# Attention and feed-forward in float32: TensorE products split into two row halves of 64, with the units' products in another order

## The chip, the cores and the metric

The kernel runs on one core of one Trainium2 chip. The metric is device time in microseconds (us). TensorE is called PE here, its weight loads PEld, VectorE DVE, ScalarE ACT, GpSimd POOL, and SyncE, which only issues DMAs in this kernel, SP. A letter q behind an engine's name means its queue.

## The reference, cut to what matters

All arrays are float32; x is 8 x 1024 x 128 (8 batches).

```python
xn = layernorm(x)                                   # per row, eps 1e-5
Q = einsum('bnd,hdk->bhnk', xn, proj_q)             # 8 heads
K = einsum('bmd,dk->bmk', xn, proj_k)               # one key and one value head for all
V = einsum('bmd,dv->bmv', xn, proj_v)
weights = softmax(einsum('bhnk,bmk->bhnm', Q, K), axis=-1)
O = einsum('bhnm,bmv->bhnv', weights, V)
Y = einsum('bhnv,hdv->bnd', O, proj_o)
mid = einsum('amh,ehn->aemn', xn, w1)               # 8 experts, no nonlinearity
ffn = einsum('aemn,enh->amh', mid, w2)
out = x + Y + ffn
```

## The kernel before

The program folds weights once, at its start: `wqk` = proj_q[h] proj_k^T, `wvo` = proj_v proj_o[h]^T, and `wf`, the sum of w1[e] w2[e]. What is left per batch is, for each head, logits = xn wqk xn^T, a softmax, and weights times (xn wvo).

**Units and steps.** A unit u is one head of one batch (64 units). A step i is 128 query rows of a unit, so a unit has 8 steps and the program 512, in the loop at L772. In step i the loop issues, in this order for each engine:

- PE: the logits of step i, 128 x 1024 in two halves (`logits`, L362), into one of two PSUM buffers of the pool `ps_sc`, which are taken in turn. Later in the step, from i = LAG = 12 on, products of an older unit (`run`, L793). Every eighth step the queries of the next unit (`queries`, L802, into `ps_sc` too), and four steps later a quarter of the values of a coming group of four units (`values`, L804, the same).
- DVE: the row maximum of step i (L354), then the 32 x 32 block transpose of the weights of step i-1 (`weights_t`, L377), then the reciprocal of step i's row sums (L370).
- ACT: the exponential of step i out of PSUM (L360), the division (L371), and the copies of queries and values out of PSUM (L305, L323, L324).
- SP: after every fourth transpose, 16 DMAs (L405) that move 32-row blocks between partitions, so that keys come to lie on partitions. The first four steps of a unit give `g0[u]` (two buffers), the last four `g1[u]` (one buffer). Each DMA fills 32 partitions of one of four query blocks; the order is block by block, and within a block the partitions from 0 up.

**The products.** Weights times values is done in a scheme with seven products of half matrices in place of eight. With x1, x2 the two key halves of g0 and y1, y2 those of g1, POOL forms f1 = x1 + x2 (`sum_early`, L423, into a buffer of the tag f), then x1 = y1 - x1 (L428, in place), x2 = f1 - y1 (L429, in place) and f4 = y2 - x2 (L431, tag f). On the values' side seven forms lie in `vfs`, four of them differences that POOL makes (L327 to L330). Each of the seven products is 64 output columns wide and runs over four key blocks c (`product`, L435), into one of four PSUM accumulators, in its lower or upper 64 partitions. `pair` (L461) issues two products that fill both halves of one accumulator: j = 0, 1 is product 4 (weights x2 of before any difference), j = 2 to 5 are the products 2 and 1 (of y2 and y1), j = 6 to 9 are 7 and 5 (x1 and f1), j = 10 to 13 are 6 and 3 (the last x2 and f4). So a unit has 14 pairs. `PAIRS` says how many run in a step: 2, 2, 1, 2.

With n = (i - 12) mod 8 and v = (i - 12) // 8, pairs j = 0, 1 of unit v run at n = 0, j = 2, 3 at n = 1, and so on. The transposes that complete g0 of unit v+1 are issued at n = 0, those that complete its g1 at n = 4. `sum_early` of unit v+1 is issued at n = 6, the three later forms of unit v at n = 0.

**Column halves.** All products that are 128 columns wide are split by `both_halves` (L100) into two of 64 columns, the same width as the products above. Every float32 product leaves two matmul and two weight load records in the trace.

Of the kernel before, what the change touches and what calls it, by code (L numbers as in the profile page):

```python
# [17 lines left out]
def kernel(  # L18
# [78 lines left out]

    banks, pwf = [0], []

    def both_halves(dst, lhsT, rhs, start=True, stop=True):  # L100
        for half in range(2):
            r = ts(half, HP)
            nc.tensor.matmul(dst[r], lhsT=lhsT[:, r], rhs=rhs, start=start, stop=stop)  # L103

# [7 lines left out]

    xs, xns, xnTs, qTs, vfs = {}, {}, {}, {}, {}

# [30 lines left out]
    TURNED = NQ * NB * Q * GN  # L145
    VF = GN * 7 * HC * HP
    s_q = scratch("turned", TURNED)
# [3 lines left out]
    wqT, wvT = wqvT[:, :H], wqvT[:, H]  # L151
    s_v = scratch("vf", VF, batch)
    wo, woT = blocks(s_v[:, : H * P]), blocks(s_v[:, H * P : 2 * H * P])
# [35 lines left out]

    lo, hi = slice(0, HP), slice(HP, P)  # L190
    wqk = const.tile([P, H, P], F32, tag="wqk", name="wqk")
# [5 lines left out]

    def transposed(dst, srcs, name, copy):  # L200
# [94 lines left out]

    def queries(u, first=0, last=S, copy=nc.scalar.copy):
        b, h = divmod(u, H)
        if first == 0:
            qTs[u] = work.tile([P, S], F32, tag="qT", name=f"qT_{u}")
        n = last - first  # L300
        pq = slot(f"pq_{u}") if n == S else bank(f"pq_{u}_{first}")
        for c in range(0, n, GS):
            w = min(GS, n - c)
            both_halves(pq[:, c : c + w], wqk[:, h, :], xnTs[b][:, first + c : first + c + w])
        copy(qTs[u][:, first:last], pq[:, :n])  # L305

    def values(s, c, copy=nc.scalar.copy):

        b, k = divmod(s, 2)
        if c == 0:  # L310
            vfs[s] = batch.tile([P, GN, 7, HC, HP], F32, tag="vf", name=f"vf_{s}")
        vf = vfs[s]
        if s == 0:
            pv = [bank(f"pv_{s}_{c}_{g}") for g in range(2)]
        else:
            both = slot(f"pv_{s}_{c}")
            pv = [both[:, ts(g, GS)] for g in range(2)]
        for g in range(2):
            both_halves(pv[g], xnTs[b][:, ts(c + g * HC, P)], wvo[:, ts(k, GN), :])
        v1, v2 = (t.rearrange("p (h j x) -> p h j x", h=GN, j=2) for t in pv)  # L320
        b11, b21, b22, t4, t1, t2, t3 = (vf[:, :, f, c] for f in range(7))
        b12 = t1
        nc.scalar.copy(vf[:, :, 0:5:4, c], v1)  # L323
        copy(vf[:, :, 1:3, c], v2)  # L324

        def differences(copy):
            nc.gpsimd.tensor_sub(t3, b22, b12)  # L327
            nc.gpsimd.tensor_sub(t1, b12, b11)
            nc.gpsimd.tensor_sub(t2, b22, t1)
            nc.gpsimd.tensor_sub(t4, b21, t2)  # L330

        deferred.append(differences)
        if copy != defer:
            flush(copy)

    sums, es, turned, g0s, g1s, f1s, f4s = {}, {}, {}, {}, {}, {}, {}

    pls, spare = {}, []  # L340

    def logits_half(i, g):
        u, n = divmod(i, NB)
        if g == 0:
            pls[i] = slot(f"pl_{i}")
        both_halves(
            pls[i][:, ts(g, GS)], qTs[u][:, ts(n, P)], xnTs[u // H][:, ts(g, GS)]
        )

    nmaxs = {}  # L350
# [10 lines left out]

    def logits(i):  # L362
        logits_half(i, 0)
        logits_half(i, 1)
        row_max(i)
        exponents(i)
# [17 lines left out]
    def move_blocks(k):  # L384
        src = turned.pop(k)
        u, g = divmod(k, 2)
        if u < B * H - 1 or g == 1:
            f = g if u < B * H - 1 else 0
            dst = work.tile(
                [P, NQ, NB, GN, Q], F32, tag=f"g{f}", name=f"g{g}_{u}", bufs=2 - f  # L390
            )
        else:
            spare.append(scratch("vf", VF, batch))
            dst = spare[0][:, :TURNED].rearrange(
                "p (r c t q) -> p r c t q", r=NQ, c=NB, t=GN
            )
        (g1s if g else g0s)[u] = dst

        def ends_of(r, d):
            return dst[ts(d, Q), r], src[ts(r, Q), d]  # L400

        for r in range(NQ):
            for d in range(NQ):
                if d != r or k < NS // GN - 1:
                    nc.sync.dma_start(*ends_of(r, d))  # L405
        if k == NS // GN - 1:
            for r in range(NQ):
                (nc.scalar.copy if r else nc.vector.tensor_copy)(*ends_of(r, r))
# [4 lines left out]
    def form(name, u):  # L413
        return work.tile([P, NQ, HC, GN * Q], F32, tag="f", name=f"{name}_{u}")

    def sum_early(u, engine):
        if u < B * H - 1:
            f1s[u] = form("f1", u)
        else:
            f1s[u] = spare[0][:, TURNED : TURNED + TURNED // 2].rearrange(  # L420
                "p (r c x) -> p r c x", r=NQ, c=HC
            )
        engine.tensor_add(f1s[u], key_half(g0s[u], 0), key_half(g0s[u], 1))  # L423

    def sums_late(u, engine):
        x1, x2 = key_half(g0s[u], 0), key_half(g0s[u], 1)
        y1, y2 = key_half(g1s[u], 0), key_half(g1s[u], 1)
        engine.tensor_sub(x1, y1, x1)  # L428
        engine.tensor_sub(x2, f1s[u], y1)  # L429
        f4s[u] = form("f4", u)  # L430
        engine.tensor_sub(f4s[u], y2, x2)  # L431

    accs = {}

    def product(u, p, c):  # L435
# [3 lines left out]
        x1, x2 = key_half(g0s[u], 0), key_half(g0s[u], 1)  # L439
        y1, y2 = key_half(g1s[u], 0), key_half(g1s[u], 1)  # L440
        acc, half, f, w = {
# [3 lines left out]
            4: (3, c // 2, 3, x2),  # L445
            5: (1, 1, 4, f1s[u]),
            6: (2, 0, 5, x2),
            7: (1, 0, 6, x1),
        }[p]
        first, last = (0, HC - 1) if p != 4 else (2 * half, 2 * half + 1)  # L450
        if (b, acc) not in accs:
            accs[b, acc] = ps_acc.tile([P, GS], F32, tag=f"acc{acc}", name=f"acc{acc}_{b}")
        nc.tensor.matmul(  # L453
            accs[b, acc][ts(half, HP)],
            lhsT=vfs[u // GN][:, u % GN, f, c, :],
            rhs=w[:, :, c, :],
            start=(h == 0 and c == first),
            stop=(h == H - 1 and c == last),
        )

    def pair(u, j):  # L461

        if j < 2:
            product(u, 4, j)
            product(u, 4, j + 2)
        else:
            k, c = divmod(j - 2, HC)
            for p in ((2, 1), (7, 5), (6, 3))[k]:
                product(u, p, c)

# [7 lines left out]

    def ffn(b, k):

        xn0, xn1 = xnTs[b][:, :GS], xnTs[b][:, GS:]
        terms = (
            ((0, lo, xn1), (1, hi, xn0)) if k == 0 else ((3, lo, xn0), (2, hi, row_diffs.pop(b)))
        )
        for acc, half, rows in terms:
            nc.tensor.matmul(  # L486
                accs[b, acc][half],
                lhsT=wf[:, half],
                rhs=rows.rearrange("d (t r q) -> d r t q", t=GN, q=Q),
                start=False,  # L490
                stop=False,
            )

    def in_order(t):
# [240 lines left out]

    PAIRS = (2, 2, 1, 2)
    LAST_PAIRS = (2, 2, 1, 1, 1, 1, 1, 1, 1, 1, 1, 0)
    COLLECT = {0: [0], 2: [1], 3: [2, 3], 4: [4], 6: [5], 7: [6, 7, 8], 8: [9], 10: [10], 11: [11]}

# [11 lines left out]
    LAST = B * H - 1  # L751
    for u in range(LAST - 2):
        jobs.extend((pair, u, j) for j in range(14))
        if u % H == H // 2 and u // H < B - 1:
            jobs.extend((ffn, u // H, k) for k in range(2))

    jobs.extend((pair, LAST - 2, j) for j in range(11))
    jobs.extend((pair, LAST - 1, j) for j in range(2))
# [8 lines left out]
    def run(n):  # L767
        for _ in range(n):
            job, *args = jobs.pop()
            job(*args)  # L770

    for i in range(NS):  # L772
        m = i % GN
        if i == 1:
            exponents(1)
        elif i > 1:
            logits(i)
        for task in early.get(i, ()):
# [8 lines left out]

        v, n = divmod(i - LAG, NB)
        if n == 6 and 0 <= v + 1 < LAST - 1:
            sum_early(v + 1, nc.gpsimd)  # L790


        if i >= LAG:  # L793
            run(
                (PAIRS[m] if i < NS - LAG else LAST_PAIRS[i + LAG - NS])
                + (n == 0 and v % H == H // 2 + 1 and v // H < B - 1) * 2
            )
            if n == 0 and v < LAST - 1:
                sums_late(v, nc.gpsimd)
            elif n == 7 and v + 1 == LAST - 1:  # L800
                sum_early(v + 1, nc.gpsimd)
        if i % NB == 0 and i > 0 and i // NB + 1 < B * H:  # L802
            queries(i // NB + 1)
        if i % NB == GN and i >= LAG:  # L804
            s, r = divmod(i + 20, 32)
            if s < 2 * B:
                values(s, r // NB)

# [77 lines left out]
```

## Time and profile before

| | |
|---|---|
| time, median of 3 runs (least to most) | 1912.9 us (1912.8 to 1914.85) |
| span of the profiled execution | 1911.0 us |
| median less span | 1.9 us |
| granted TensorE clock | 1.000 |
| PE busy, matmul records | 1905.4 us, 8994 |
| DVE, ACT, POOL busy | 1410.2, 1356.1, 1402.1 us |
| DMAs of L405: issues, us from issue to landing | 2044, 2.4 (median) |
| starts of the logits of n = 4, 5, 6, 7 and the next n = 0, 1, in order of time | 1010.12, 1015.27, 1018.71, 1021.28, 1024.71, 1029.87 us |

The profiled execution is one run; its span goes from the first to the last instruction, and the runs' times are a little longer than a span. In the rows quoted below, a matmul row gives line, engine, output <- inputs and sizes (128*64 is 128 rows of the array by 64 columns). The end of a matmul is modelled, its start is recorded; a row of 0.592 us is 0.429 us of streaming, after which the next one of the same column half starts, and 0.163 us in which the last results come out. Square brackets at the end of a row tell how long the engine was idle before it and what ended that.

### The profile page before, as it was taken

What the parts mean: (1) busy time and instruction counts of PE and PEld (TensorE: products, weight loads), DVE (VectorE), ACT (ScalarE), POOL (GpSimd) and SP (SyncE); (2) the same over time, 40 slices, a digit from 0 to 9 for tenths busy, and PEclk for the clock granted to TensorE, in tenths of its full rate; (3) what the DMA queues carried; (4) which work ended last, traced back from release to release, by engine and by line L of the source; (5) the groups of instructions that cost most, each with busy time, mean ns of one, the idle gap of its engine ahead of it and who ended that gap; (6) DMA issues with size and microseconds to landing.
All of it is one profiled execution on the core that took longest, in us unless ns stands there. A gap on an engine that the chain in (4) does not pass through costs nothing.

```text
span 1911.0 us, 26803 instructions
## 1 busy us (share of the span) xinstructions
PE 1905.4 (100%) x8994; PEld 646.3 (34%) x8994; DVE 1410.2 (74%) x1779; ACT 1356.1 (71%) x1823; POOL 1402.1 (73%) x592
## 2 busy tenths in 40 slices
PE   9999999999999999999999999999999999999999
PEld 4333333333333333333333333333333333333333
DVE  8767778677786777777777776777678766787777
ACT  7677677776776777777676777777777776777674
POOL 2877877688676886777967768777687777677763
PEclk9999999999999999999999999999999999999999
DMA  6666676676767766677667776776767667666675
GB/s 200 155 154 148 143 155 153 144 171 150 158 141 156 171 150 147 151 159 167 145 147 158 158 166 138 157 158 144 179 139 156 149 148 173 137 144 146 155 174 133
DMA packets 140713, 295.07 MB, mean 154 GB/s; under 512 B 41120, under 2 KB 74656, under 8 KB 140064
## 3 DMA queue, kind: packets, MB, share of 16 engines
q1 hardware_dynamic: 139744, 292.96, 68.2%
q8 instruction: 72, 1.18, 0.3%
q14 instruction: 65, 0.53, 0.1%
q10 hardware_dynamic: 832, 0.39, 0.1%
HBM read 13.76 MB, written 4.19 MB: 9 GB/s over the span
## 4 chain that ended last, share of the span: by engine, by line
PE 78%; POOL 9%; SPq 5%; DVE 3%; ACT 2%; DMA 2%; issue 1%; POOLq 0%; DVEq 0%
PE pl L103 37%; PE acc L453 32%; SPq L405 5%; PE pq L103 4%; PE pv L103 4%; POOL f L431 2%; POOL g L428 2%; POOL g L429 2%; DMA g<-turned 2%; DVE nmax L354 1%; ACT e L360 1%; DVE turned L377 1%; PE acc L486 1%; ACT e L371 1%; DVE scratch_vf L224 0%
## 5 line engine op out<-in xcount | busy, mean ns | idle before, releaser
L103 PE MATMUL pl<-xnT,qT 128*64 128x512 f32 x4096 | 966.5, 592 | 0.5 <-DVE xnT L294 0.2
L354 DVE TENSOR_REDUCE nmax<-pl 128x1 f32<-128x1024 f32 x512 | 626.3, 1223 | 403.6 <-PE pl L103 402.6
L360 ACT ACTIVATE e<-pl,nmax 128x1024 f32<-128x1024 f32 x512 | 570.1, 1113 | 399.9 <-DVE nmax L354 399.9
L453 PE MATMUL acc<-g,vf 128*64 128x512 f32 x2536 | 843.3, 592 | 0.0
L371 ACT ACTIVATE e<-e,rinv 128x1024 f32<-128x1024 f32 x512 | 588.1, 1149 | 116.5 <-DVE rinv L370 116.4
L377 DVE STREAM_TRANSPOSE turned<-e 128x1024 f32<-128x1024 f32 x512 | 633.8, 1238 | 13.7 <-ACT e L371 2.2
L103 PEld LDWEIGHTS pl<-xnT,qT 128*64 128x64 f32 x4096 | 292.8, 137 | 585.5 <-issue 534.3
L453 PE MATMUL acc<-f,vf 128*64 128x512 f32 x1016 | 487.2, 592 | 0.0
L428 POOL TENSOR_TENSOR g<-g,g 128x2048 f32<-128x2048 f32 x63 | 287.1, 4558 | 260.8 <-DMA g<-turned 127.1
L453 PEld LDWEIGHTS acc<-g,vf 128*64 128x64 f32 x2536 | 247.6, 137 | 506.5 <-issue 503.9
L423 POOL TENSOR_TENSOR f<-g 128x2048 f32<-128x2048 f32 x63 | 287.2, 4558 | 174.3 <-PE acc L453 86.2
L431 POOL TENSOR_TENSOR f<-g,g 128x2048 f32<-128x2048 f32 x63 | 287.8, 4569 | 4.9
L429 POOL TENSOR_TENSOR g<-f,g 128x2048 f32<-128x2048 f32 x63 | 286.9, 4554 | 0.0
L453 PEld LDWEIGHTS acc<-f,vf 128*64 128x64 f32 x1016 | 139.2, 137 | 0.0
L103 PE MATMUL pq<-xnT,wqk 128*64 128x512 f32 (+1 forms) x516 | 121.5, 589 | 0.1
L103 PE MATMUL pv<-wvo,xnT 128*64 128x512 f32 x512 | 120.8, 592 | 0.0
L370 DVE RECIPROCAL rinv<-sums 128x1 f32<-128x1 f32 x512 | 83.8, 164 | 42.9
L360 ACT ACTIVATION_READ_ACCUMULATOR e<-pl,nmax 128x1 f32 x512 | 98.3, 192 | 0.0
L327 POOL TENSOR_TENSOR vf<-vf 128x256 f32<-128x256 f32 x64 | 46.9, 733 | 31.1 <-ACT vf L324 31.1
L305 ACT COPY qT<-pq 128x1024 f32<-128x1024 f32 (+2 forms) x66 | 63.6, 963 | 0.0
L103 PEld LDWEIGHTS pv<-wvo,xnT 128*64 128x64 f32 x512 | 37.2, 137 | 72.7 <-issue 69.4
L103 PEld LDWEIGHTS pq<-xnT,wqk 128*64 128x64 f32 x516 | 36.9, 137 | 71.9 <-issue 71.3
(100 smaller groups left out, 534.0 us busy)
## 6 DMA issues: line engine op xcount, KB each, us to landing
g<-turned SPq DMA_DIRECT2D x2028, 128.0 KB, 2.4
xn<-in_L_attn_x_dram SPq DMA_DIRECT2D x7, 512.0 KB, 4.6
xnT<-xnt SPq DMA_DIRECT2D x112, 32.0 KB, 1.9
out<-yt SPq DMA_DIRECT2D x112, 32.0 KB, 1.9
x<-in_L_attn_x_dram SPq DMA_DIRECT2D x6, 512.0 KB, 4.2
out_dram<-x SPq DMA_DIRECT2D x6, 512.0 KB, 5.1
scratch_g<-in_L_ffn_w_dram SPq DMA_DIRECT2D x2, 1024.0 KB, 8.4
scratch_f<-in_L_ffn_w_dram SPq DMA_DIRECT2D x2, 1024.0 KB, 12.6
```

The lines of the kernel that those rows point to most:

```text
L103: nc.tensor.matmul(dst[r], lhsT=lhsT[:, r], rhs=rhs, start=start, stop=stop)
L354: nc.vector.reduce_max(nmaxs[i], pls[i], AX.X, negate=True)
L360: nc.scalar.activation(es[i], pl, AF.Exp, bias=nmax, accum_out=sums[i])
L370: nc.vector.reciprocal(rinv, sums.pop(i))
L371: nc.scalar.mul(es[i], es[i], rinv)
L377: nc.vector.transpose(turned[k].rearrange("p k c t q -> p c k t q")[:, :, :, j, :], es.pop(i).rearrange("p (c k q) -> p c k q", k=NQ, q=Q),)
L405: nc.sync.dma_start(*ends_of(r, d))
L423: engine.tensor_add(f1s[u], key_half(g0s[u], 0), key_half(g0s[u], 1))
L428: engine.tensor_sub(x1, y1, x1)
L429: engine.tensor_sub(x2, f1s[u], y1)
L431: engine.tensor_sub(f4s[u], y2, x2)
L453: nc.tensor.matmul(accs[b, acc][ts(half, HP)], lhsT=vfs[u // GN][:, u % GN, f, c, :], rhs=w[:, :, c, :], start=(h == 0 and c == first), st ...
```

## The change

PE gets 64-row halves of every product in the steady steps (i = 15 to 499). A product of 128 rows becomes one of the lower 64 rows (start flag as before) and one of the upper 64 that is added to it in PSUM. `couple` issues one half of the rows of two things at a time: the upper rows of one and the lower rows of the other, which write different PSUM banks. At its second call for the same key, it issues the other halves. Ahead of each such call, from the third on, PE gets an instruction that waits until the call before the last one has finished.

```diff
+    def halves(dst, lhsT, rhs, start=True, stop=True):
+        return [(dst[r], lhsT[:, r], rhs, start, stop) for r in (ts(0, HP), ts(1, HP))]
+    def half_rows(job, r, first):
+
+        for dst, lhsT, rhs, start, stop in job:
+            done = nc.tensor.matmul(
+                dst, lhsT=lhsT[r], rhs=rhs[r], start=start and first, stop=stop and not first
+            )
+        return done
+
+    begun, slots = {}, []
+
+    def couple(key, jobs):
+
+        if len(slots) > 1:
+            wait = nc.tensor.nop()
+            tc.add_manual_dep(wait.ins, slots[-2].ins.name, AFTER, reason="other rows of a bank")
+        if key not in begun:
+            begun[key] = jobs
+            half_rows(jobs[1], hi, True)
+            slots.append(half_rows(jobs[0], lo, True))
+        else:
+            a, b = begun.pop(key)
+            half_rows(b, lo, False)
+            slots.append(half_rows(a, hi, False))
```

`queries`, `values`, `logits_half`, `product`, `pair` and `ffn` are rewritten to return lists of such jobs, which `whole` issues as before (used in steps 0 to 14 and from 500 on). In the steady steps the order is

```diff
+    PAIRS = {
+        0: ((0, 2), (-1, 11)),
+        1: ((0, 3), (-1, 12)),
+        2: ((0, 4), (-1, 13)),
+        3: ((0, 5), (0, 6)),
+        4: ((0, 7), (1, 0)),
+        5: ((0, 8), (1, 1)),
+        6: ((0, 9), (0, 10)),
+    }
+    FIRST_PAIRS = (0, 2), (1, 3), (4,)
...
+        def products(own):
+            if n < 7:
+                pairs = [pair_job(v + d, j) for d, j in PAIRS[n]]
+            couple("own", own)
+            if n == 7 and other is None:
+                couple("pairs", None)
+                couple("own", None)
+                return
+            couple("other" if n == 7 else "pairs", other if n == 7 else pairs)
+            couple("own", None)
+            if n == 7:
+                couple("other", None)
+            elif other is not None:
+                couple("other", other)
+                couple("pairs", None)
+                couple("other", None)
+            elif n < 6 or (v % H == H // 2 + 1 and v // H < B - 1):
+                couple("pairs", None)
```

where (d, j) is pair j of unit v + d, `own` is the two halves of the step's logits, and `other` is the values (n = 0), the queries (n = 4) or, once a batch, the feed-forward products (n = 7). The second halves of a pair may so come after the second halves of the logits, and the pairs of n = 6 end at n = 7. The first pairs of unit v+1 (product 4) now run at n = 4 and 5 of unit v, those of y1 and y2 at n = 0 to 3, and the last three pairs of unit v-1 at n = 0 to 2 of unit v. A step's row maximum and exponential are issued after all of this.

The forms follow that order:

```diff
     def sum_early(u, engine):
-        if u < B * H - 1:
+        if in_place(u):
+            f1s[u] = key_half(g0s[u], 1)
+        elif u < B * H - 1:
             f1s[u] = form("f1", u)
...
     def sums_late(u, engine):
...
-        engine.tensor_sub(x1, y1, x1)
-        engine.tensor_sub(x2, f1s[u], y1)
-        f4s[u] = form("f4", u)
-        engine.tensor_sub(f4s[u], y2, x2)
+        if not in_place(u):
+            engine.tensor_sub(x1, y1, x1)
+        f2s[u] = form("f2", u) if in_place(u) else x2
+        engine.tensor_sub(f2s[u], f1s[u], y1)
+        f4s[u] = form("f4", u)
+        engine.tensor_sub(f4s[u], y2, f2s[u])
+
+    def sum_middle(u, engine):
+        x1, y1 = key_half(g0s[u], 0), key_half(g1s[u], 0)
         engine.tensor_sub(x1, y1, x1)
...
+        elif steady():
+            if n == 0:
+                sum_middle(v, nc.gpsimd)
+            elif n == 2:
+                sums_late(v, nc.gpsimd)
+            elif n == 5 and in_place(v + 1):
+                sum_early(v + 1, nc.gpsimd)
```

`in_place(u)` holds for all units but the first and the last three. f1 takes the place of x2, and what was x2 = f1 - y1 goes to a buffer of the tag f as f2. The values' forms `vfs` become two fixed tiles with the key block as the first index; which differences POOL makes is as before. In the last twelve steps the order of pairs (`LAST_PAIRS`) and of the reads of the accumulators (`COLLECT`) is shifted to start with the three pairs that are left over from before.

## The prediction

> **What bounds the kernel now.** I read the page first: busy time of the engines and the granted clock.
>
> ```profile
> PE 1905.4 (100%) x8994; PEld 646.3 (34%) x8994; DVE 1410.2 (74%) x1779; ACT 1356.1 (71%) x1823; POOL 1402.1 (73%) x592
> ...
> PEclk9999999999999999999999999999999999999999
> ```
>
> PE is busy for 1905.4 of 1911.0 us, and the table of matmul groups gives it 0.5 us of idle time ahead of the logits (L103 pl). A busy PE may still hide gaps, so I looked at its weight loads and its matmuls in order of time, in the step that starts at 1010.12 (start us, us, engine, line, operation).
>
> ```profile
> 1010.12 1.89 PE L103 MATMUL pl<-xnT,qT 128*64 128x512 f32 x8
> 1011.84 0.59 PE L453 MATMUL acc<-g,vf 128*64 128x512 f32 x1
> 1011.85 0.59 PE L453 MATMUL acc<-f,vf 128*64 128x512 f32 x1
> 1012.27 0.59 PE L453 MATMUL acc<-g,vf 128*64 128x512 f32 x1
> 1012.28 0.59 PE L453 MATMUL acc<-f,vf 128*64 128x512 f32 x1
> ...
> 1013.56 1.89 PE L103 MATMUL pq<-xnT,wqk 128*64 128x512 f32 x8
> 1015.27 1.89 PE L103 MATMUL pl<-xnT,qT 128*64 128x512 f32 x8
> ```
>
> Every product leaves two records (4096 logits records for 512 steps of four products of 64 columns). Two records of different column halves start 0.01 us apart, and the next two 0.429 us later. So eight records take 1.716 us (1010.12 to 1011.84), gaplessly: PE streams at a fixed pitch. Then I followed one half of the softmax weights from the logits to POOL (DVE, SP and POOL in the same stretch).
>
> ```profile
> 1012.22 1.23 DVE L354 TENSOR_REDUCE nmax<-pl 128x1 f32<-128x1024 f32 x1
> 1013.48 1.25 DVE L377 STREAM_TRANSPOSE turned<-e 128x1024 f32<-128x1024 f32 x1
> ...
> 1014.86 10.04 SPq L405 DMA_DIRECT2D g<-turned  x16
> ...
> 1027.13 4.57 POOL L428 TENSOR_TENSOR g<-g,g 128x2048 f32<-128x2048 f32 x1 [4.47 <-DMA g<-turned]
> ```
>
> The transpose that completes a half stands on DVE behind the same step's row maximum. It ends at 1014.72; sixteen DMAs follow, 0.63 us apart on SP; POOL, which waits for them, starts 12.4 us after the transpose. This half is g1, and its first product comes at 1031.58, 4.5 us after it has landed. g0 has longer. That margin is what I watch.
>
> **The change, part by part.** Durations are those of the profiled execution (span 1911.0 us); the median of the runs shown, 1912.9, is 1.9 above, and I carry that along.
>
> *The matmuls.* Each product becomes two of 64 rows, so 64-row records double and weight loads too. Call one call of couple a slot: half the rows of two products, eight records of the 64 x 64 kind. No row here shows row halves. Below, nothing in the trace gives a pitch shorter than 0.429 for two records, so a slot takes 2 x 0.429 = 0.858 us if its four quarters run side by side; above, 1.716 if the row halves take turns. I take 0.858, since column halves, the nearest row, do run side by side. PE's work per unit is then unchanged: 34 slots (6 in n=0 and n=4, 4 in n=1, 2, 3, 5, 3 in n=6 and 7), 34 x 0.858 = 29.17 us, just what 136 records cost before.
>
> The Trainium skill (FP8 and Floating Point Precision, TensorE Precision Notes) says that true fp32 takes four passes through the array; with the 2.4 GHz of its page TensorE: Matmul & The Clock Gate (table at the top) that makes 853 ns for 128 x 128 x 512, an estimate, and the trace's two pitches, 858 ns, agree, so by it there is nothing to win in streaming. The same skill (TensorE: Matmul & The Clock Gate, Part 3) tells of four row tiles that ran 3.07 times as fast, not four; by that share a slot would take some 1.12 us and the kernel some 2450 us, an estimate that no run here shows.
>
> *Doubled weight loads.* A load takes 0.137 us, and two start together. Four beside each other cost nothing; one after the other they take 0.55 us against a pitch of 0.43, so a slot would be 1.10 us and a unit 37.3. I take nothing.
>
> *The waits.* Ahead of each slot PE waits for the slot before the last one. That slot ends 0.592 - 0.429 = 0.16 us after its streaming, while the next one still has 0.7 us to stream, and the semaphore instruction is a 51 ns row of which some 600 stand in the trace with PE idle for under 1 us. I take nothing; if PE's queue did not run ahead, 34 x 0.21 = 7.3 us a unit, 440 us in all.
>
> *The PSUM slots of the logits.* The second half of a step's logits is now a slot of pairs later, so the step's rows end 2.57 us after it starts, not 1.72. From there: 0.21 to the maximum, 1.22, 0.04, exponential 1.11, 0.14 until PE runs again (least gap in the trace): 2.72 us. At n=1, n=5 and the next n=0 the buffer wanted is that of the step before, 3 slots = 2.57 us after it was filled: 0.15 us late each. These lie ahead of the next two waits and vanish in them.
>
> *The order of the units' products* is the dearest part. The transposes that complete g0[u] and g1[u] stay in the steps n=0 and n=4 of unit u-1, but their first products move: product 4 of u from n=0 of u to n=4 of u-1, the products of y1 and y2 from n=1 to n=0. Both are now four steps after the transpose. From a pairs slot P1 that had to wait, the path to the next one is: P1 and second half of the logits 2 x 0.858 = 1.72; 0.21; maximum 1.22; 0.03; transpose 1.24; landing 12.4: 16.8 us. PE has 18 slots from P1 of n=0 to P1 of n=4, 15.44 us: **1.35 us late**. From P1 of n=4 to that of the next n=0 it has 16 slots, 13.73 us; there the first product in need takes the lower 64 rows, which the first 14 DMAs fill, 2 x 0.63 earlier: 15.5 us, **1.76 late**. A unit costs 29.17 + 3.1 = 32.3. If PE waits for all sixteen there, 1.3 more.
>
> Sum: 61 times 1.35, 60 times 1.76, less 1.7 in each of the seven units that have two ffn slots at n=7 in the way: 82 + 106 - 12 = 176 us. 1911.0 + 176 + 1.9 = 2089, say **2090 us**.
>
> *POOL and SP.* POOL keeps its four forms of 4.56 us. f2 and f4 now start after n=2 of their unit (f2's buffer is read until then) and end at 1.8 + 12.0 + 9.1 = 22.9 us of the unit; g1 has one buffer, whose next DMAs want to start at 23.9. The cover is 1.0 us; each us beyond it moves the landing. They are used at 28. x1, in place, is done 4.6 us after g1 has landed, at 8.6, and used at 14.6. f1 in place frees a buffer and costs nothing. SP has 16 x 0.63 = 10 us in 14: it doesn't queue. The last twelve steps keep whole products and the first pairs at step 12 come after the landing: nothing.
>
> **Rivals.**
> 1. *The row halves take turns.* A slot is 1.716, a unit 58.3: 1913 + 61 x 29.2 = 3690 us. For it: no row shows 64-row tiles beside each other. Against: column halves do it. Between lie serialised weight loads (1913 + 61 x 8.1 = 2410) and bare waits (2355); here landings are hidden again (PE alone decides from a slot of 0.95 us).
> 2. *The landing is no wait*: DMAs land earlier, or the transpose doesn't stand behind the maximum. Then the 0.15 us of the PSUM slots remain, 0.45 a unit: 1940 us, or no change at 1913 if they go too. Against: the 12.4 us are measured, and POOL's wait for them is a row (127 us in total).
> 3. *Faster: 64-row tiles stream quicker.* Place: every slot; price 34 x 61 = 2074 slots, so each 0.01 us less is worth 21 us, if nothing waits. By the path above a unit is 28.8 + 4 slots, which at half the pitch is still 30.5, or 1995 us. Faster than before only if slots shrink below 0.85 and the landings also come 3 us a unit earlier: 29.17 must be undercut. 1880 us if both held and slots took 0.84.
>
> **How the numbers follow.** Landing waits as worked out, 2000 to 2200: 0.57. Dearer slots, 2200 to 2420: 0.12. Turns, 3690: 0.09. Landing mostly hidden, 1917 to 2000: 0.10. Within 0.2%: 0.05. Faster: 0.07. 0.2% is about what a measurement of this kernel can tell from no change. The likeliest is 2090; 1930 to 2400 takes in the sixteen-DMA bound (2170), bare waits and nearly all of the serialised loads, and leaves out turns, no change and faster, 0.2 together.
>
> **What would show it.** Right: matmul records nearly doubled, four with starts within some 0.03 us and 0.43 us between such groups; PE idle of 1 to 2 us ahead of products that read g, put down to the DMAs g<-turned, about twice a unit, some 170 us in all; DVE, ACT and POOL busy as before; units 32 us apart. Wrong: groups of two with 0.43 us between them (turns); PE idle ahead of every slot (bare waits); loads one after another; or no idle and 29.2 us a unit. POOL's f4 ending after the transpose of n=4 would make the landing wait longer than I have it.

## The result, and the profile after

The changed kernel takes **2190.1 us** (median of 4 runs, 2187.07 to 2195.35), beside 1913.1 for the kernel before (1912.8 to 1914.85, 4 runs): 1.1448 times as long, interval 1.1432 to 1.1465. The forecast was 2090, with a range of 1930 to 2400. The direction and the mechanism were right; the loss is 277 us where 176 were worked out. The profiled execution has a span of 2185.3 us, 274.3 more than before, and those 274 us are what is accounted for below.

The page after, busy times and the chain that ended last:

```profile
PE 2028.7 (93%) x17282; PEld 737.7 (34%) x17282; DVE 1415.7 (65%) x1779; ACT 1356.2 (62%) x1823; POOL 1403.8 (64%) x592
...
SPq 40%; PE 36%; DMA 12%; issue 5%; DVE 5%; POOL 1%; ACT 1%; DVEq 0%; POOLq 0%
```

DVE, ACT and POOL do what they did before, and PE's records have nearly doubled. What bounds the kernel has changed, as the chain of before shows beside it: there PE had 78% and SP's queue 5%; now SP's queue has 40% and the DMAs' landing 12%.

```profile
PE 78%; POOL 9%; SPq 5%; DVE 3%; ACT 2%; DMA 2%; issue 1%; POOLq 0%; DVEq 0%
```

PE's matmuls in order of time, in a stretch of step n=0 to 1 without a wait (start us, us, engine, line, operation):

```profile
1214.27 0.60 PE L117 MATMUL acc<-f,vf 64*64 64x512 f32 x2
1214.29 0.60 PE L117 MATMUL acc<-g,vf 64*64 64x512 f32 x2
1214.70 0.60 PE L117 MATMUL acc<-f,vf 64*64 64x512 f32 x2
1214.71 0.59 PE L117 MATMUL acc<-g,vf 64*64 64x512 f32 x2
1215.13 1.04 PE L117 MATMUL pl<-xnT,qT 64*64 64x512 f32 x8
1215.99 0.59 PE L117 MATMUL acc<-g,vf 64*64 64x512 f32 x2
```

Four quarters of the array start within 0.02 us, the next four 0.43 us later, and a slot of eight records takes 0.86 us (1214.27, 1215.13, 1215.99). So the row halves run side by side, at the pitch of before.

Then the path from one waiting product to the next, in the timeline of all engines (g0, the half that is used at n=4):

```profile
1207.12 1.02 PE L117 MATMUL acc<-f,vf 64*64 64x512 f32 x4
...
1208.83 0.65 PE L117 MATMUL acc<-g,vf 64*64 64x512 f32 x2 [0.69 <-DMA g<-turned]
...
1210.85 1.22 DVE L409 TENSOR_REDUCE nmax<-pl 128x1 f32<-128x1024 f32 x1 [1.92 <-PE pl L117]
...
1211.99 1.23 DVE L435 STREAM_TRANSPOSE turned<-e 128x1024 f32<-128x1024 f32 x1
...
1213.29 10.95 SPq L463 DMA_DIRECT2D g<-turned  x16
...
1226.12 1.09 PE L117 MATMUL acc<-g,vf 64*64 64x512 f32 x8 [1.37 <-DMA g<-turned]
```

From product to product (1208.83 to 1226.12) it is 17.29 us, where the forecast had 16.8; PE has 15.44 us of work for that stretch. The sixteen issues on SP take 10.95 us here and took 10.04 in the stretch of before that the prediction shows.

The groups of instructions give the sum of such waits ahead of products that read g:

```profile
L117 PE MATMUL pl<-xnT,qT 64*64 64x512 f32 x7760 | 1066.5, 597 | 3.3
L117 PE MATMUL acc<-g,vf 64*64 64x512 f32 x4856 | 890.5, 595 | 143.6 <-DMA g<-turned 127.4 <-issue 8.0 <-DVE rinv L428 3.8
```

143.6 us look like less than 274. They are idle time of the whole of PE, and in a waiting slot of n=0 two quarters have other work: only the rows of g wait, while those of the other pair, which are issued first (the row at 1207.12), go ahead. So the 1.71 us from 1207.12 to 1208.83 count as 0.69 us of idle time, and PE's "busy" 2028.7 us hide the rest. The sure measure is the distance from one row maximum to the next, since each follows its logits directly:

| from step to step | slots x 0.858 | before | after | difference from PE's work |
|---|---|---|---|---|
| n=1 to 2, 2 to 3, 5 to 6 | 4 = 3.43 | (other order) | 3.43 | 0 |
| n=0 to 1 and n=4 to 5 | 6 = 5.15 | 5.31, 5.32 | 5.40, 5.43 | 0.25, 0.28: PSUM buffer |
| n=3 to 4 | 4 = 3.43 | 3.43 | 5.23 | 1.80: g0 |
| n=6 to 7 | 3 = 2.57 | (other order) | 2.68 | 0.11: one more slot in the seven units with ffn |
| n=7 to 0 | 3 = 2.57 | 3.39 | 4.63 | 2.06: g1, and the same ffn slot |
| sum of a unit (mean) | | 29.44 | 33.66 | 4.22 more than before |

The steps of before hold other products, four slots from n=7 to 0 for example, so its rows compare with the changed kernel's only in the sum.

### The profile page after: what moved, and what is told of

It reads as the page before. It is cut to its first block, busy times and chain, and to the rows that moved or that the text cites. A ratio compares the mean times of both kernels' runs of the same rounds, so it can differ in the third digit from the quotient of the medians.

```text
span 2185.3 us, 44147 instructions
## 1 busy us (share of the span) xinstructions
PE 2028.7 (93%) x17282; PEld 737.7 (34%) x17282; DVE 1415.7 (65%) x1779; ACT 1356.2 (62%) x1823; POOL 1403.8 (64%) x592
## 3 DMA queue, kind: packets, MB, share of 16 engines
q8 instruction: 140, 2.29, 0.5%
## 4 chain that ended last, share of the span: by engine, by line
SPq 40%; PE 36%; DMA 12%; issue 5%; DVE 5%; POOL 1%; ACT 1%; DVEq 0%; POOLq 0%
SPq L463 40%; PE acc L117 15%; DMA g<-turned 12%; PE pl L117 11%; PE pv L117 6%; PE pq L117 2%; DVE nmax L409 2%; DVE turned L435 2%; PE pl L109 1%; PE acc L109 0%; ACT e L429 0%; ACT e L415 0%; POOL f L496 0%; POOL g L492 0%; POOL g L494 0%
## 5 line engine op out<-in xcount | busy, mean ns | idle before, releaser
L117 PE MATMUL pl<-xnT,qT 64*64 64x512 f32 x7760 | 1066.5, 597 | 3.3
L117 PE MATMUL acc<-g,vf 64*64 64x512 f32 x4856 | 890.5, 595 | 143.6 <-DMA g<-turned 127.4
L117 PE MATMUL acc<-f,vf 64*64 64x512 f32 x1928 | 501.8, 589 | 0.0
L117 PEld LDWEIGHTS pl<-xnT,qT 64*64 64x64 f32 x7760 | 301.5, 133 | 585.7 <-issue 414.4
L486 POOL TENSOR_TENSOR g<-g 128x2048 f32<-128x2048 f32 x60 | 273.6, 4561 | 292.9 <-PE acc L117 275.3
L117 PEld LDWEIGHTS acc<-g,vf 64*64 64x64 f32 x4856 | 241.2, 133 | 510.9 <-issue 375.5
L496 POOL TENSOR_TENSOR f<-g,f 128x2048 f32<-128x2048 f32 x60 | 271.8, 4530 | 4.7
L117 PEld LDWEIGHTS acc<-f,vf 64*64 64x64 f32 x1928 | 139.5, 133 | 155.1 <-issue 121.2
L117 PE MATMUL pv<-wvo,xnT 64*64 64x512 f32 x944 | 173.1, 596 | 0.0
L117 PE MATMUL pq<-xnT,wqk 64*64 64x512 f32 x976 | 132.2, 599 | 0.0
```

The costliest lines, as they stand in the source:

```text
L117: done = nc.tensor.matmul(dst, lhsT=lhsT[r], rhs=rhs[r], start=start and first, stop=stop and not first)
L496: engine.tensor_sub(f4s[u], y2, f2s[u])
```

## The experiments

Each time is the median of its runs beside runs of the kernel before on the same chip (1913.1 to 1913.7); "waits at n=4 and n=0" are read as in the table above. A DMA issue of SP has a median of 0.59 us in every kernel; one over 0.8 us is called long.

### e1: the new order, whole rows

```diff
-            begun[key] = jobs
-            half_rows(jobs[1], hi, True)
-            slots.append(half_rows(jobs[0], lo, True))
+            begun[key] = (jobs, fresh)
+            whole(jobs[fresh])
...
-            half_rows(b, lo, False)
-            slots.append(half_rows(a, hi, False))
+            whole(js[1 - k])
```

Here `fresh` picks the first pair, at n=4 the pair of product 4.

> The new order of products with whole rows of 128: no row halves, no added waits, matmul records back to about 9,000. Theory A (the order puts each landing on the path, and doubled instruction fetches lengthen it): PE still waits about twice a unit for the DMAs that move g. With the landing of before (12.4 us) the wait at n=4 is 16.8 - 15.44 = 1.35 us as forecast, and at n=0 it is 16.8 - 13.73 = 3.1 us, since a whole product needs all sixteen DMAs; 61 x 4.4 = 270 us on 1913, and some 10 for the start and the end: 2160 to 2230 us, by chance about the time of the changed kernel. SP's long issues and the instruction packets go back to about 62 and 72. Rival B (row halves or the waits ahead of each slot cost the time): 1913 to 1940 us.

Measured: **2242.5 us**, ratio 1.1723 (1.1681 to 1.1764). Without any row half and any added wait the kernel is slower still, so B falls: the order costs the time. The waits are 1.22 us at n=4 and 3.45 at n=0, 4.67 together where 4.4 were expected; the time is 12 us above the upper end. The surplus shows in PE's clock. Busy times by window, with the granted clock behind POOL's column, and PE's matmuls in the middle window:

```profile
1016.63:1023.46 6.83, 4.90 (x22) 1.20 (x18) 5.45 (x8) 5.29 (x9) 5.68 (x2) 1.00 0.77 169
1023.46:1030.29 6.83, 5.08 (x12) 1.65 (x14) 1.36 (x2) 0.99 (x2) 4.51 (x1) 0.50 0.12 26
1030.29:1037.10 6.81, 6.81 (x34) 2.50 (x32) 3.44 (x4) 4.21 (x6) 2.90 (x4) 1.00 0.63 140
```

```profile
1025.21 1.98 PE L109 MATMUL acc<-g,vf 128*64 128x512 f32 x4 [3.68 <-DMA g<-turned]
1026.94 1.95 PE L109 MATMUL pl<-xnT,qT 128*64 128x512 f32 x4
1028.65 1.86 PE L109 MATMUL pv<-wvo,xnT 128*64 128x512 f32 x4
1030.33 1.04 PE L109 MATMUL acc<-f,vf 128*64 128x512 f32 x4
```

After a wait of 3.68 us the next three slots take 1.68 to 1.73 us in place of 0.86: the clock is at half. Over the whole execution it is at half for 126 us (32 stretches, mean clock 0.972), at most 63 us of lost streaming; in the changed kernel for 27 us.

### e2 and e9: the new order with twice as many instructions

Two ways to cut a matmul in two without row halves. e2 cuts the 512 columns at 256, e9 takes the first and the second 64 queries of each of the four query blocks:

```diff
+            for k in range(2):
                 for dst, lhsT, rhs, start, stop in job:
...
-                nc.tensor.matmul(dst, lhsT=lhsT, rhs=rhs, start=start, stop=stop)
+                    nc.tensor.matmul(
+                        strip(dst, k),
+                        lhsT=lhsT,
+                        rhs=strip(rhs, k),
+                        start=start and k == 0,
+                        stop=stop and k == 1,
+                    )
```

> The kernel of the run before with each matmul of the steady steps cut into two of 256 columns, so that PE's instructions double, without row halves and without added waits. Theory A: about 140 instruction packets, about 110 long SP issues, each landing some 0.6 us longer than in the run before, so 1.2 us a unit, 50 to 90 us more than that run, if a matmul of 256 columns streams in half the time of one of 512. Rival B (instruction fetches don't touch SP; row halves are what made the landing longer): the time and the long issues of the run before. If the pitch of the smaller matmuls is longer than 0.215 us, PE's own work grows, and that part is to be taken off first.

Measured: **2223.5 us** (1.1632, 1.1596 to 1.1667): neither theory's number, but 19 us less than e1. SP did what A said (143 packets, 82 long issues where e1 has 32, the sixteen issues 0.38 to 0.40 us longer at each landing). Why the time fell all the same I could only argue: the first 256 columns read two query blocks, which the first eight DMAs fill, so half of the first product runs before the landing ends. e9 takes that way out:

> Again the new order with whole rows and each matmul cut into two, but the weights' products are cut so that both parts read all four query blocks (the first and the second 64 queries of each), so that the first part can't start before all sixteen DMAs, as it could in the run with two blocks each (there the first part needed eight). Theory A (doubled instructions lengthen SP's sixteen issues, and that lengthens the time): about 140 packets, 80 to 110 long issues, each landing 0.4 us longer than with uncut products, 61 x 0.8 = 49 us and 11 us for the pitch of the smaller matmuls (as the kernel before showed it when it was cut): 2275 to 2325 us beside 2242 for the uncut order. Rival B (the longer issues don't reach the time): 2235 to 2260 us.

Measured: **2294.6 us** (1.2007, 1.1981 to 1.2033), 52 us above e1, as A had it (60), and beyond B. 141 packets, 84 long issues, each landing 0.37 to 0.41 us longer than in e1. Some 11 of the 52 us are the pitch (3.45 us for four slots in place of 3.43). The waits grew from 1.22 and 3.45 us to 1.48 and 3.89, 0.70 together, which times 58 units is about the other 41 us. The clock was at half for 169 us, 43 more than in e1; the half clock that follows a wait is part of these distances, so how much of the 41 us is the clock's is not taken apart.

### e3: the kernel before, with twice as many instructions

The same cut at 256 columns, in `both_halves` and `product` of the kernel before.

> The kernel before, in its own order, with each matmul of the loop cut into two of 256 columns: PE's instructions double. Theory A: about 140 instruction packets in place of 72, about 110 long SP issues in place of 62, the sixteenth issue some 0.5 us later after the transpose; the time stays at 1913 us within 0.3%, since there the landing has 4.5 us to spare. Rival B (fetches and long issues only happen to fall together): packets double and long issues stay near 62. If the smaller matmuls stream slower, the time grows by that alone.

Measured: **1924.2 us** (1.0059, 1.0044 to 1.0074). The time is outside the 0.3%, by the pitch: a unit takes 29.35 us in place of 29.18, times 64 is 11 us. On SP the theory held. With e1, e9 and the changed kernel:

| kernel | instruction packets | long SP issues | first to sixteenth issue, mean us, g0 and g1 |
|---|---|---|---|
| before | 72 | 62 | 9.85, 9.76 |
| before, cut (e3) | 142 | 109 | 10.03, 10.21 |
| new order, whole (e1) | 72 | 32 | 9.78, 9.64 |
| new order, cut (e9) | 141 | 84 | 10.15, 10.05 |
| changed kernel | 140 | 111 | 10.28, 10.14 |
| changed kernel, only pairs in halves (e10) | 101 | 82 | 9.98, 10.02 |

The packets are rows of the table of DMA queues, of before and of after:

```profile
q8 instruction: 72, 1.18, 0.3%
```

```profile
q8 instruction: 140, 2.29, 0.5%
```

Each is 16 KB. That they are PE's instructions is read from their number, which doubles with PE's records (8994 matmuls and as many loads before, 17282 of each after). In the changed kernel 108 of 111 long issues fall together in time with such a packet, in the kernel before 57 of 62; of the other issues it is 53 of 2199 and 32 of 2248. The doubling in e3 and e9, with nothing else changed for SP, makes this more than a coincidence. How many packets meet an issue depends on the order too: e1 has the 72 packets of before and only 32 long issues. Where landings have time to spare (e3) it costs nothing, where they set the end (e9) it does.

### e4: three quarters of the moved blocks

```diff
             for d in range(NQ):
+                if r == NQ - 1 and steady() and 3 < u < B * H - 1:
+                    continue
                 if d != r or k < NS // GN - 1:
```

The tiles of g0 and g1 are then kept from unit to unit.

> The changed kernel, with row halves, waits and order as they are, but in the steady steps the four DMAs of the last of the four query blocks are left out (that block keeps an older unit's weights), so twelve DMAs move each half. Theory A: the landing is 4 x 0.63 = 2.5 us shorter, which is more than the wait at n=4 (some 2.0 us) and at n=0 (some 2.3 us): the waits for g go, the short ones for PSUM buffers (0.19 us, three a unit) stay, 1913 + 35 and some for the start and the end: 1935 to 1970 us. Rival B (row halves, the doubled weight loads or the added waits cost the time): 2150 to 2190 us, since none of them is touched.

Measured: **1991.4 us** (1.0405, 1.039 to 1.0421). B falls: with row halves, doubled loads and waits all there, 199 of the 277 us are gone. The waits for g are 0.03 us at n=4 and some 0.2 at n=0. The group of products that read g has 16.1 us of idle time in place of 143.6, and the chain that ended last is PE's again:

```profile
L117 PE MATMUL acc<-g,vf 64*64 64x512 f32 x4856 | 877.8, 590 | 16.1 <-DMA g<-turned 13.1 <-POOL g L496 1.9 <-issue 1.1
...
PE 90%; SPq 3%; ACT 2%; DVE 1%; POOL 1%; DMA 1%; issue 1%; ACTq 0%; DVEq 0%; POOLq 0%
```

It is 21 us above the upper end. A unit is 30.31 us where before had 29.44: the waits for PSUM buffers are 0.25 us, not 0.19, at n=1, n=5 and n=0, and 61 x 0.87 = 53; the rest are the first two units and the last steps, which stay as slow as in the changed kernel.

### e5: lower rows first at n=4

```diff
-        4: ((0, 7), (1, 0)),
+        4: ((1, 0), (0, 7)),
```

> The changed kernel with the two pairs of n=4 swapped, so that the first slot of product 4 takes the lower 64 rows of g0, as the first slot of n=0 does with g1. Theory A (the first product waits for the last DMA of those rows that it reads): the wait at n=4 then ends with the fourteenth DMA, not the sixteenth, some 1.28 us earlier in each of 61 units: 78 us less, about 2110 us (2090 to 2140), and the wait at n=0 is as before. Rival B (PE waits for a whole transfer, or for something else that ends there): 2190 us.

Measured: **2120.8 us** (1.1079, 1.1062 to 1.1095), 69 us less by swapping two pairs of one step. A's number; B falls. The wait at n=4 fell from 1.80 to 0.41 us, and the one at n=0 rose from 2.06 to 2.29. The idle time of the group:

```profile
L117 PE MATMUL acc<-g,vf 64*64 64x512 f32 x4856 | 935.5, 595 | 62.7 <-DMA g<-turned 53.9 <-issue 4.8 <-POOL g L492 2.2
```

So each product waits for the DMAs of its own rows and no more: the first product starts 2.6 us after the sixteenth issue at n=4 of the changed kernel, and 2.6 us after the fourteenth at n=0.

### e7: the DMAs of the lower partitions first

```diff
-        for r in range(NQ):
-            for d in range(NQ):
+        for d in range(NQ):
+            for r in range(NQ):
                 if d != r or k < NS // GN - 1:
```

> The run with the two pairs swapped, and the sixteen DMAs in another order: the partitions outside, the query blocks inside, so that the first eight fill the lower 64 partitions of all four blocks. Theory A: the first slot waits for eight DMAs, 13 - 8 issues or some 3.2 us earlier than in the run before, and the slot that needs all sixteen comes three slots, 2.57 us, later. At n=4 nothing is late, at n=0 some 1.1 us: 1913 + 67, with the waits for PSUM buffers and the start and end 2000 us (1970 to 2040). Rival B (the sixteen DMAs must all be there before any product starts): 2110 to 2190 us.

Measured: **2008.3 us** (1.0498, 1.048 to 1.0515), as A had it, with everything moved and computed. No wait is left at n=4 (3.44 us for its 3.43), 0.07 us at n=0 beside the PSUM buffer's 0.26, and from n=0 to 1 it is 5.93 us: the slot with the upper rows, 0.78 us late with the PSUM wait in it. The group, with 5.8 us of its idle time put down to the DMAs:

```profile
L117 PE MATMUL acc<-g,vf 64*64 64x512 f32 x4856 | 932.6, 591 | 14.3 <-DMA g<-turned 5.8 <-issue 3.1 <-POOL g L492 2.2
```

### e6 and e8: transposes ahead of the maximum

```diff
+        if ahead(i):
+            weights_t(i - 1)
         nmaxs[i] = small.tile([P, 1], F32, tag="nmax", name=f"nmax_{i}")
```

`ahead` is true in the steady steps with n=0 and n=4.

> The changed kernel with the transposes that complete a half put ahead of the row maximum of the same step on DVE, in the steps n=0 and n=4. Theory A (the path runs from one waiting product through the end of the logits, the maximum and the transpose to the next landing): the transpose no longer waits for the logits of a step that was itself delayed. It can start after the division of the step before, some 4.3 us after that step's logits, so the two waits of a unit together fall from some 4.4 to some 2.0 us: 2045 us (2010 to 2100). Rival B (PE's waits come from the row halves or from SP alone): 2190 us or more, since the maximum now comes later.

> Both together: transposes ahead of the maximum in n=0 and n=4, the DMAs of the lower 64 partitions first, and the lower rows first in n=4. Theory A: what is late at n=0 falls from 1.1 to some 0.4 us and nothing at n=4; with the waits for PSUM buffers 1930 to 1980 us, and not under 1911, since PE's work is 29.17 us a unit as before. Rival B: row halves would also save streaming time once nothing waits: below 1900 us.

Measured: **2211.3 us** (1.1554, 1.1537 to 1.1571) and **2210.0** (1.1549, 1.1532 to 1.1566). Both numbers of A were wrong by 160 us and more. B's number fits e6, and so does its remark that the maximum now comes later; what it says of the waits does not, and e8's B (below 1900) falls too. The waits for g are nearly gone, and a new one has their place. The group of logits and of products, idle time and releaser last:

```profile
L117 PE MATMUL pl<-xnT,qT 64*64 64x512 f32 x7760 | 1043.2, 599 | 183.9 <-ACT e L415 182.7
L117 PE MATMUL acc<-g,vf 64*64 64x512 f32 x4856 | 890.1, 595 | 17.2 <-DMA g<-turned 13.4 <-POOL g L497 2.2 <-issue 0.7
```

And one such step in the timeline:

```profile
1103.48 1.23 DVE L409 TENSOR_REDUCE nmax<-pl 128x1 f32<-128x1024 f32 x1 [0.77 <-PE pl L117]
...
1104.74 1.12 ACT L415 ACTIVATE e<-pl,nmax 128x1024 f32<-128x1024 f32 x1 [0.85 <-DVE nmax L409]
...
1106.18 1.15 ACT L434 ACTIVATE e<-e,rinv 128x1024 f32<-128x1024 f32 x1 [0.23 <-DVE rinv L433]
...
1107.36 1.25 DVE L440 STREAM_TRANSPOSE turned<-e 128x1024 f32<-128x1024 f32 x1 [1.22 <-ACT e L434]
...
1108.53 1.19 DVE L409 TENSOR_REDUCE nmax<-pl 128x1 f32<-128x1024 f32 x1
1109.75 1.11 ACT L415 ACTIVATE e<-pl,nmax 128x1024 f32<-128x1024 f32 x1 [2.42 <-DVE nmax L409]
...
1111.01 1.09 PE L117 MATMUL pl<-xnT,qT 64*64 64x512 f32 x8 [1.59 <-ACT e L415]
```

The maximum of a step now stands behind the maximum, exponential, reciprocal, division and transpose of the step before: 1103.48 to 1108.53 is 5.05 us, for steps in which PE has 3.43 (n=3 to 4) or 2.57 us (n=7 to 0) of work. PE waits for the PSUM buffer that this late exponential frees. 1.62 + 2.47 = 4.1 us a unit is about what the landings had cost. In e8 landings are out of the way altogether, and the unit is the same 33.69 us (median of both): in these two steps the chain over DVE and ACT alone sets the time. The order of the changed kernel, maximum first, is the better one.

### e10: row halves only in the pairs

```diff
+        if key != "pairs":
+            if key not in begun:
+                begun[key] = jobs
+                slots.append(whole(jobs[0]))
+            else:
+                slots.append(whole(begun.pop(key)[1]))
```

> The changed kernel in its order, but the logits, queries, values and feed-forward products keep whole rows, one job in each slot; only the pairs are split into row halves. PE has 26042 instruction words in place of 35834. Theory A: packets 100 to 105 in place of 140, long issues 75 to 90 in place of 111, each landing 0.15 to 0.25 us shorter, 61 x 0.4 = 24 us less: 2150 to 2180 us. Rival B (the number of instructions is nothing; row halves of the logits cost something): 2185 to 2195 us by the first half of it, below 2130 by the second.

Measured: **2216.1 us** (1.1584, 1.1568 to 1.16). Packets and long issues came as expected; the time did not, by 36 us, for a reason neither theory had. PE's matmuls:

```profile
1203.98 1.09 PE L118 MATMUL acc<-g,vf 64*64 64x512 f32 x8
1205.00 1.08 PE L109 MATMUL pl<-xnT,qT 128*64 128x512 f32 x4
1206.01 1.09 PE L118 MATMUL acc<-g,vf 64*64 64x512 f32 x8
1207.02 1.08 PE L109 MATMUL pl<-xnT,qT 128*64 128x512 f32 x4
```

Slots of halved and of whole rows take turns, and each takes 1.01 us in place of 0.86 without any wait. Four such slots are 4.06 us, three 2.89: 0.157 us at each change between 64 and 128 rows. That is close to the 0.163 us in which a record's last results come out after its streaming; that the next rows wait for these results is not shown. 28 changes a unit are 4.4 us, which makes PE the bound again (it is busy 2194.6 of 2213.8 us) and hides the landings, all but some 0.4 us at n=0. So this run says nothing on what the instruction count costs in time; e9 does.

## Why the prediction was right in kind and short in size

**The slot, 0.858 us** with four quarters side by side: right, to the hundredth (3.43 us for four slots, in every kernel that halves all rows). The Trainium skill (TensorE: Matmul & The Clock Gate, Part 3) has four row tiles at 3.07 times the speed, by which the estimate was 2450 us. Here four quarters, two of rows by two of columns, lose nothing. The rival of turns (3690) is out, and so is a gain in streaming.

**Doubled weight loads and the waits ahead of each slot, nothing:** right. Four slots with four waits and 32 loads take 3.43 us, and e4 leaves all of them in and is 199 us faster.

**PSUM buffers, 0.15 us three times a unit:** 0.25, 0.25 and 0.26. They vanish in the landing waits, as forecast, because the path and not PE's work sets the unit; e4 and e7 show them uncovered.

**POOL's cover of 1.0 us:** held. SP issues the first DMA of g1 0.15 us after the transpose, as before, so f4 is out of the way in time.

**Which DMA releases what, and the two late products:** right, sixteen at n=4 and fourteen at n=0, shown by e5 and e7. Also the rule that a wait passes its lateness on: the two paths together are the unit.

**The landing, 12.4 us: this term was mis-sized.** From the end of the transpose to the first product it measured 13.1 us at n=4 (0.19 to the first issue, 10.29 to the sixteenth, 2.64 to the product, means over 59 units) and 11.8 at n=0, for which I had 11.1. So each path is some 0.7 us longer than I put it, one time at n=4 and one at n=0; the rest of the paths is as worked out. The cause is SP's sixteen issues (10.29 and 10.15 us from the first to the last). I took them from one clean stretch, 15 x 0.63 = 9.5 us. The mean in the same trace was 9.8, since an issue is now and then long; and doubling PE's instructions doubled their fetches and brought the mean to 10.2. About half of the miss could have been read in the trace of before, by taking all landings and not one. The other half is an effect of the change that no step of mine had: PE's instructions were costed on PE alone. That more instructions lengthen the issues is shown by e3 and e9, that a longer landing is lost time by e4, e5 and e7.

In us of the profiled execution: 58 steady units lost 246 where the forecast gives 168 (58 x 3.1 less 12), so 78 more. The first two units lost 18 and the last steps 10, where it left some 8 in all for them: 20 more. 168 + 78 + 8 + 20 = 274. In the first steady unit PE stood 8 us, at 111.92, for a landing, and then ran at half clock; a filling pipeline was not among my steps, and of these 28 us no experiment takes the parts apart.

**The clock** was in no step of the forecast: full in the profile of before, and at half for 27 us after, at most 14 us, 10 of the 27 in the first unit and at the very end. It is inside the sums above. In e1 and e9 it is a term of its own.

What stays open: why a fetch of PE's instructions holds up an issue on SP. The runs show that it does, not where the two meet.

No variant of the new order comes near 1913 us. Row halves leave PE's work at 29.17 us a unit, and before the change PE already worked without a gap.

## What to carry to other kernels

Halving rows didn't make these float32 products, which used the whole array, any faster: four quarters streamed as much as two halves did. When a reordering moves a product nearer to the transfer that feeds it, write the loop from one waiting product to the next and fill it with means over all its instances; a loop longer than the work between its ends is the new time, and moving one link of it (as in e6) may only close another loop elsewhere. Before any larger cure, look which DMAs a product really reads: swapping two pairs gave 69 us, and turning the order of sixteen DMAs 112 more.

## What the runs showed of the hardware that was not expected

- **PE's instruction stream slows SP.** An issue of 0.59 us becomes some 1.5, in most cases, when a 16 KB packet of PE's instructions is fetched at the same time: 62 long issues with 72 packets, 109 with 142, in the same order of work (e3).
- **The clock halves after waits of about 2 us.** In the changed kernel five stretches of 1.94 to 2.35 us without streaming were each followed by 3.41 us at half clock, while most of that size were not. Cut into stretches of 3.41 us, the next one was at half when matmuls streamed for less than some 0.4 of the time, and at full when for more (the two overlap between 0.37 and 0.43, in the changed kernel, e1 and e6). In e5 and e7 a stretch at 0.50 was followed by half clock too, so 0.4 is no sharp border. The Trainium skill (TensorE: Matmul & The Clock Gate, Part 1) tells of the same free-running window of 3413 ns, and of half rate after an idle window. In these runs a window that was 0.4 busy was idle enough.
- **Changing between 64 and 128 rows costs 0.157 us each way** (e10). The Trainium skill (TensorEngine Tiling (Array Packing), Key Properties) says that changing the tiling mode drains the engine. The 0.157 us fit that, but no run shows the drain by itself.
